# Gated attention with routed experts on one core: the first batch's queries by seven block products, their key-side sums on GpSimd, and bf16 products in a short wait

## The chip, the cores and the metric

The kernel runs on one core of one Trainium2 chip. Times are device microseconds (us). The median of several runs is what counts; beside it there is one profiled execution, from which all durations below are taken. Engines are named as in the profile: PE is TensorE (matmul), PEld its weight load, DVE is VectorE, ACT is ScalarE, POOL is GpSimd, SP is SyncE. "L555" is line 555 of the kernel.

## The reference

The input is x, 2 batches of 1024 tokens with 512 features, f32. Two branches start from the same layer norm, and their product is added to x:

```python
xn = _layernorm(x, axis=-1)
qkv = einsum('bsh,oh->bso', xn, w_qkv) + b_qkv          # attention, one head of 512
scores = einsum('bqh,bkh->bqk', q, k) / sqrt(512)
s = (softmax(scores) @ v) @ w_out.T + b_out
logits = xn @ router_w + router_b                       # 8 experts, the best 2 per token
h = einsum('td,edf->etf', xn, expert_w) + expert_b
combined = sum over the 2 experts of weight * silu(h)
y = xn + combined @ proj_w + proj_b
g = silu(norm_w * y / rms(y))
out = x + s * g
```

## The kernel before

**Algebra.** Scores are not made from queries and keys. The product of the two weight matrices, `wqk`, is made once (`product`, L580 on), queries are `xn` times `wqk` plus a column `u`, and the keys are `xn` itself, transposed (`xnT`, one tile for each batch). Value and output weights are multiplied together beforehand (`product_vo`), so `vo` holds values that already carry the output weights. Biases become small terms: `u` (from the query bias, through `sk`), a column of the router matrix `rw` (from the key bias, through `sq` and the products `pw`), and `vb`, the value bias times the output weights, which is added to `bo`. `weighted` makes the vectors `sq`, `sk` and `vb` as four scaled 128x512 slices summed on VectorE; `columns`, or a product with `ones`, then sums over partitions.

**Stages, in order of time.**
1. Loads; the value weights' product; layer norm of 16 token tiles (`means`, `variances`, `norm`, `turn_x`); in a loop over tiles t, `value_half` gives values and router logits. Inside that loop, at given t, stand `turn_w` (t = 8), `sk` (9), `vb` (10), `u` (11), `pvb` and the closing of the pool of raw weights (12) and the issue of the expert weights `ew` (13): 16 transfers on SP's queue and 16 on GpSimd's.
2. Routing, about 91 to 121 us: VectorE finds the two best experts of each token (`first_max`), counts tokens per expert (`both`, `upto`, `before`), gives each a row (products `pk`, `prank`), and builds one-hot tables `hsel`, `tsel`, `lsel`, whose products `ptok` give each expert slot's list of tokens, `tok`. TensorE does the products of `wqk` and the first batch's queries (`queries`, four calls) between these.
3. Experts: 39 slots of 128 tokens. Each slot is gathered (`xg`, GpSimd), put to memory and taken back (`xs`, `sz`, SP), transposed (`gT`, VectorE), multiplied (`ph`), its expert's bias `eb` added (VectorE) and passed through silu (ScalarE). The steps run ahead of a slot's product by 7, 5, 3 and 1 slots; `xg` and `sz` have four buffers, `gT` two.
4. Attention for pairs of 128 queries, already with seven block products instead of eight (`pair_scores`, `attend`).

**Order.** The order written in the program holds on every engine (`keep_order`): an instruction that waits holds up all that is written behind it on its engine. `hold(n)` writes n bf16 products of 128x256 that nothing reads. PSUM has four one-bank tiles `ps_mm` and two two-bank tiles `ps_big`.

Of the kernel before, what the change touches and what calls it, by code (L numbers as in the profile page):

```python
# [27 lines left out]
def kernel(  # L28
# [200 lines left out]
    for q in range(4):  # L229
        for j in range(KC):  # L230
            gps.tensor_copy(bqk[ts(q, QP), :, j], bqkv[ts(j, QP), 0:2, q])  # L231
    spread(gps, wZ[0], w_qkvT[:, ts(0, H)], others)
    load_x(gps, others, 2, 2)
# [4 lines left out]
    load_x(gps, others, 4, 4)  # L238
    ln_eps = const.tile([P, 1], FP, name="ln_eps")
    gps.memset(ln_eps, LN_EPS)  # L240
    rms_eps = const.tile([P, 1], FP, name="rms_eps")
    gps.memset(rms_eps, RMS_EPS)
# [3 lines left out]
    ones = const.tile([P, P], FP, name="ones")  # L246
    gps.memset(ones, 1.0)

    rb = const.tile([P, E1], FP, name="rb")
# [69 lines left out]

    def weighted(w_, bias, name):  # L320

        s_ = raw.tile([P, H], FP, tag="s", name=name, bufs=3)
        for c in range(KC):
            b_ = bias[:, c : c + 1]
            if c:
                dve.scalar_tensor_tensor(s_, w_[:, c, :], b_, s_, ALU.mult, ALU.add)
            else:
                dve.tensor_scalar(s_, w_[:, c, :], b_, None, ALU.mult)
            yield s_
# [63 lines left out]
    def turn_x(t):  # L393
        turn(xnT[t // ST][:, :, ts(t % ST, P)], x[:, t], "(i a)")
# [40 lines left out]
    norm(0)  # L435
    norm(1)
    turn_w(wqkT[:, 0:KC], wZ[0])
    product_vo(1, 0)
    turn_x(0)
    turn_x(1)  # L440
# [43 lines left out]
    pbb = ps_mm.tile([P, 512], FP, tag="mm", name="pbb")  # L484
    pe.matmul(pbb[:, 0:KC], lhsT=ones, rhs=bb, start=True, stop=True)
    dve.tensor_reduce(rb[:, E:E1], pbb[:, 0:KC], AX.X, ALU.add)
    dve.tensor_copy(rw[:, :, E], columns(sq_, "pw"))
    value_half(0, 0)
    turn_x(2)
# [10 lines left out]
    for t in range(2, NT):  # L500
# [17 lines left out]
        if t == 2:  # L518
            gps.dma_start(bo, b_out.partition_broadcast(P))
        if t == 8:  # L520
            turn_w(wqkT[:, KC:], wZ[1])
        if t == 9:
            *_, sk_ = weighted(wqkT[:, KC:], bqk[:, 0], "sk")
        if t == 10:

            *_, vb = weighted(wo, bqkv[:, 2], "vb")
        if t == 11:
            dve.tensor_copy(u, columns(sk_, "pu"))
        if t == 12:
# [15 lines left out]
    close(ln_guard)  # L545
    eb_guard, ebp = pool("eb", side="right")
    eb = ebp.tile([P, E, H], FP, name="eb")
    sp.dma_start(eb, expert_b.partition_broadcast(P))

    def queries(oc):  # L550

        ps = ps_big.tile([P, SH, 512], FP, tag="big", name=f"pq{oc}")
        for half in range(SH):
            for c in range(KC):
                pe.matmul(  # L555
                    ps[:, half, :],
                    lhsT=wqk[:, c, ts(oc, P)],
                    rhs=xnT[0][:, c, ts(half, 512)],
                    start=(c == 0),
                    stop=(c == KC - 1),  # L560
                )
        act.activation(
            qT[:, :, oc, :],
            ps.rearrange("p a (k f) -> p (a k) f", f=PW),
            AF.Identity,
            bias=u[:, oc : oc + 1],
        )

# [129 lines left out]
    product(3)  # L698
    queries(0)
    pt_ = ps_mm.tile([P, 512], FP, tag="mm", name="ptok")  # L700
    LG = 8
    for g in range(2 * NT // LG):
        lsel = rt.tile([P, LG, P], BF, tag="lsel", name=f"lsel{g}", bufs=4)
        dve.tensor_tensor(
            lsel,
            mixed.rearrange("p a i -> p (a i)").unsqueeze(1).to_broadcast([P, LG, P]),
            flat(lo)[:, ts(g, LG)].unsqueeze(2).to_broadcast([P, LG, P]),
            ALU.is_equal,
        )
        for j in range(LG):  # L710
            i = g * LG + j
            pe.matmul(
                pt_[:, : 2 * NSP],
                lhsT=lsel[:, j, :],
                rhs=tsel[:, i].rearrange("p k s -> p (k s)"),
                start=(i == 0),
                stop=(i == 2 * NT - 1),
            )
    tk = rt.tile([P, 2, NSP], FP, name="tk")
    dve.tensor_copy(tk.rearrange("p k s -> p (k s)"), pt_[:, : 2 * NSP])  # L720
# [22 lines left out]
    close(rt_guard)  # L743
    queries(1)
    pm = ps_mm.tile([P, 512], FP, tag="mm", name="pm")
# [6 lines left out]
    close(rc_guard)  # L752
    for oc in range(2, KC):
        queries(oc)

# [97 lines left out]

    for s in range(-steps[0][1], NS):
        pipeline(steps, s, NS)
        if LR <= s < LR + NT:
# [21 lines left out]

    KH = KC // 2
    SK = ST // 2  # L880
# [482 lines left out]
```

## Time and profile before

| what | value |
|---|---|
| median of 3 runs | 539.74 us (539.64 to 541.14) |
| the profiled execution | 540.82 us |
| its span, first to last instruction | 539.1 us, mean granted TensorE clock 0.995 |
| value products (`pv`, L462) | 60.9 us busy, 256 instructions |
| products of `wqk` (`pqk`, L586) | 32 instructions, 592 ns each as recorded |
| first batch's queries (`pq`, L555) | 28.1 us busy, 64 instructions |
| drains of these to `qT` (ACT, L562) | 4 of 1113 ns |
| expert products (`ph`, L814) | 120.3 us busy |
| `eb` load (SP's queue) | 2048 KB, 15.2 us from issue to landing |
| DMA, whole span | 112.37 MB, 208 GB/s |

A f32 product is two instructions on TensorE, so the 32 query products are 64. Instructions overlap: recorded lengths of TensorE are longer than the distance from one to the next, and sums are made with the distance. The chain of waits goes back from the last instruction to what released each step; a timeline row has start, length, engine, line, operation, output and inputs, shape, count, and in brackets the idle time before it with what ended it. A row by windows has busy time and count for PE, PEld, DVE, ACT and POOL, then the granted clock, the DMA share and GB/s.

### The profile page before, as it was taken

How to read it: one execution, taken by the hardware profiler on the slowest of the kernel's cores; microseconds unless marked ns; L12 is line 12 of the kernel's file. 1: busy time of each engine (PE TensorE's matmuls, PEld its weight loads, DVE VectorE, ACT ScalarE, POOL GpSimd, SP SyncE). 2: the span in 40 equal slices, each digit the busy share in tenths (PEclk: the TensorE clock that was granted, in tenths of full speed). 3: DMA queues.
4: the chain of work that ended last, by engine and by line, in shares of the span. 5: the costliest groups of instructions: out<-in, count | busy, mean ns of one | idle time of the engine just before them, and what ended most of it. 6: DMA issues, size and time to landing. Idle time of an engine off the chain costs nothing.

```text
span 539.1 us, 5950 instructions
## 1 busy us (share of the span) xinstructions
PE 527.3 (98%) x1762; PEld 322.1 (60%) x1762; DVE 311.2 (58%) x565; ACT 167.0 (31%) x316; POOL 236.0 (44%) x272
## 2 busy tenths in 40 slices
PE   7999999999999999999999999999999999999996
PEld 5778877444444444444466656756846657484585
DVE  2565652840333333333859376375697685949586
ACT  1535562211311111111333422423426234152340
POOL 8610006022234875230227445246189755464542
PEclk9989999999999999999999999999999999999999
DMA  9995339999999999994387922723625638295512
GB/s 212 206 220 127 78 79 227 275 217 336 319 338 331 359 348 338 318 290 146 125 281 234 299 83 92 273 78 123 229 78 179 230 95 297 71 312 176 187 54 78
DMA packets 89057, 112.37 MB, mean 208 GB/s; under 512 B 6849, under 2 KB 59201, under 8 KB 88897
## 3 DMA queue, kind: packets, MB, share of 16 engines
q1 hardware_dynamic: 75072, 75.51, 47.5%
q0 software_dynamic: 8192, 26.24, 16.4%
q10 hardware_dynamic: 5760, 10.23, 5.0%
q8 instruction: 15, 0.25, 0.2%
q14 instruction: 18, 0.14, 0.1%
HBM read 70.54 MB, written 41.42 MB: 208 GB/s over the span
## 4 chain that ended last, share of the span: by engine, by line
PE 87%; DVE 6%; issue 3%; DMA 2%; POOL 1%; ACT 1%; DVEq 0%; POOLq 0%
PE ph L814 20%; PE so L1147 17%; PE pp L1076 14%; PE po L1013 10%; PE pv L462 10%; PE pq L555 5%; PE pr L574 4%; PE sc L1057 3%; PE pqk L586 3%; DMA wZ<-in_L_attn_w_qkv_dram 2%; DVE sc L1082 1%; DVE pT L120 1%; ACT x L380 1%; POOL bqk L231 1%; DVE h L840 1%
## 5 line engine op out<-in xcount | busy, mean ns | idle before, releaser
L814 PE MATMUL ph<-ew,gT 128*128 x280 | 120.3, 592 | 0.0
L814 PEld LDWEIGHTS ph<-ew,gT 128*128 128x128 f32 x280 | 53.2, 190 | 66.9 <-issue 66.9
L788 POOL DMA_INDIRECT xg<-xn_d,tok x39 | 37.3, 957 | 78.2 <-DMA xs<-xg 52.2
L840 DVE TENSOR_TENSOR h<-ph,eb 128x512 f32<-128x512 f32 x39 | 26.8, 690 | 75.6 <-issue 40.4
L462 PE MATMUL pv<-rwvo,xnT 128*128 128x256 f32 (+1 forms) x256 | 60.9, 394 | 1.8 <-DVE xnT L120 1.0
L462 PEld LDWEIGHTS pv<-rwvo,xnT 128*128 128x128 f32 x256 | 48.6, 194 | 11.2 <-ACT x L380 1.4
L843 ACT ACTIVATE h<-h 128x512 f32<-128x512 f32 x39 | 24.5, 629 | 97.7 <-DVE h L840 89.0
L1013 PE MATMUL po<-pw,ct 128*128 128x512 f32 x112 | 49.2, 592 | 0.0
L975 POOL DMA_INDIRECT hg<-ho_d,posi_m x32 | 32.4, 1013 | 37.0 <-DVE nm L1041 23.4
L1044 ACT ACTIVATE pr<-sc,nm 128x1024 f32<-128x1024 f32 x16 | 18.3, 1145 | 90.7 <-DVE nm L1041 89.0
L1154 DVE TENSOR_TENSOR o<-so,o 128x256 f32<-128x256 f32 x49 | 20.0, 421 | 38.8 <-PE so L1147 25.9
L1192 POOL TENSOR_TENSOR o<-o,base 128x512 f32<-128x512 f32 x14 | 20.6, 1493 | 45.3 <-DVE o L1157 45.3
L1076 PE MATMUL pp<-xnT,qT 128*128 128x512 f32 x84 | 39.5, 592 | 0.0
L1147 PE MATMUL so<-vo,pT 128*128 128x256 f32 x168 | 38.5, 379 | 0.0
L1013 PEld LDWEIGHTS po<-pw,ct 128*128 128x128 f32 x112 | 21.3, 190 | 25.5 <-issue 25.3
L1147 PEld LDWEIGHTS so<-vo,pT 128*128 128x128 f32 x168 | 31.9, 190 | 7.3 <-issue 2.6
L120 DVE STREAM_TRANSPOSE gT<-sz 128x512 f32<-128x512 f32 x39 | 27.4, 702 | 13.4 <-DMA sz<-xs 13.4
L1082 DVE TENSOR_TENSOR sc<-pp,sc 128x512 f32<-128x512 f32 x49 | 31.6, 679 | 5.2 <-PE pp L1076 5.2
L539 POOL DMA_DIRECT2D ew<-in_L_ffn_expert_w_dram x16 | 8.7, 551 | 57.6 <-PE pvb L531 51.2
L574 PE MATMUL pr<-xnT,wqk 128*128 128x256 f32 x128 | 28.8, 381 | 0.9 <-DVE sc L1082 0.9
L120 DVE STREAM_TRANSPOSE pT<-pz 128x1024 f32<-128x1024 f32 x14 | 28.2, 2011 | 0.2 <-DMA pz<-ps 0.2
L574 PEld LDWEIGHTS pr<-xnT,wqk 128*128 128x128 f32 x128 | 24.2, 190 | 6.6 <-DVE sc L1082 2.2
(227 smaller groups left out, 819.9 us busy)
## 6 DMA issues: line engine op xcount, KB each, us to landing
xs<-xg SPq DMA_DIRECT2D x39, 256.0 KB, 4.7
sz<-xs SPq DMA_DIRECT2D x39, 256.0 KB, 4.6
ho_d<-h ACTq DMA_DIRECT2D x39, 256.0 KB, 4.7
ps<-pr SPq DMA_DIRECT2D x16, 512.0 KB, 3.3
pz<-ps SPq DMA_DIRECT2D x16, 512.0 KB, 5.7
xn_d<-x SPq DMA_DIRECT2D x32, 128.0 KB, 2.4
ew<-in_L_ffn_expert_w_dram POOLq DMA_DIRECT2D x16, 256.0 KB, 10.9
ew<-in_L_ffn_expert_w_dram SPq DMA_DIRECT2D x16, 256.0 KB, 13.6
```

The costliest lines, as they stand in the source:

```text
L120: dve.transpose(dst.rearrange(f"p j {order} -> p i j a", a=QP), z.rearrange("p i (j b) -> p i j b", b=QP),)
L462: pe.matmul(pvs[t][:, n, : HH + E1 * (1 - n)], lhsT=xnT[t // ST][:, c, ts(t % ST, P)], rhs=rwvo[:, c, cols], start=(c == 0), stop=(c == KC ...
L555: pe.matmul(ps[:, half, :], lhsT=wqk[:, c, ts(oc, P)], rhs=xnT[0][:, c, ts(half, 512)], start=(c == 0), stop=(c == KC - 1),)
L574: pe.matmul(ps[:, :PW], lhsT=wqk[:, c, ts(oc, P)], rhs=xnT[1][:, c, ts(k, PW)], start=(c == 0), stop=(c == KC - 1),)
L788: gps.indirect_dma_start(out=xg[s], out_offset=None, in_=xn_d, in_offset=bass.IndirectOffsetOnAxis(ap=tok[:, s : s + 1], axis=0),)
L814: pe.matmul(ph, lhsT=g_[:, c, :], rhs=ew[:, ds(r, 1), c, :].rearrange("p e f -> p (e f)"), start=(c == 0), stop=(c == KC - 1),)
L840: dve.tensor_tensor(h, ph, eb[:, ds(r, 1), :].rearrange("p e f -> p (e f)"), ALU.add)
L975: gps.indirect_dma_start(out=g_, out_offset=None, in_=ho_d, in_offset=bass.IndirectOffsetOnAxis(ap=posi_m[:, n, t : t + 1], axis=0),)
L1013: pe.matmul(po, lhsT=c_[:, c, :], rhs=pw[:, c, :], start=(c == 0), stop=(c == KC - 1))
L1076: pe.matmul(ps, lhsT=l_[:, c, :], rhs=r_[:, c, :], start=(c == 0), stop=(c == KH - 1))
L1082: dve.tensor_tensor(dst, ps, other, ALU.add)
L1147: pe.matmul(ps[:, :w_], lhsT=l_[:, c, :], rhs=r_[:, c, :], start=(c == 0), stop=(c == SK - 1),)
```

## The change

The first batch's queries are a product of `wqk` (512x512) and `xnT[0]` (512x1024). Cut into 2x2 blocks, it is now made from seven block products (Winograd's form): sums S1 to S4 of blocks of `wqk` and T1 on VectorE, T2 to T4 of blocks of `xnT[0]` on GpSimd, written directly behind the routing's first op; and the seven products are joined by VectorE sums in `qT`. Six of the products stand around the routing; the seventh (the second product, `p2`) stands at the head of the expert loop: ScalarE drains it into the space of `pw`, GpSimd adds it. The sums' pool `qs` takes the space that `eb` had, so `eb` is loaded after the third product and from ScalarE's queue.

Beside that: `vb` is made on GpSimd at t = 2, with separate scalings and sums; `pvb` goes from t = 12 to 6, `sk` from 9 to 10, `u` from 11 to 12. The constants `ln_eps`, `rms_eps` and `ones` are set earlier on GpSimd. The first token tile is transposed ahead of the query weights. Two `hold`s are added around the products `pw`.

```diff
@@ constants, before the first wZ loads of GpSimd's queue
+    ln_eps = const.tile([P, 1], FP, name="ln_eps")
+    gps.memset(ln_eps, LN_EPS)
+    rms_eps = ...
+    ones = const.tile([P, P], FP, name="ones")
+    gps.memset(ones, 1.0)
     spread(gps, wZ[0], w_qkvT[:, ts(0, H)], others)
...
@@ weighted(w_, bias, name, eng=dve)
+            if not c:
+                eng.tensor_scalar(s_, w_[:, c, :], b_, None, ALU.mult)
+            elif eng is dve:
                 dve.scalar_tensor_tensor(s_, w_[:, c, :], b_, s_, ALU.mult, ALU.add)
             else:
-                dve.tensor_scalar(s_, w_[:, c, :], b_, None, ALU.mult)
+                m_ = raw.tile([P, H], FP, tag="m", name=f"{name}_m{c}", bufs=2)
+                eng.tensor_scalar(m_, w_[:, c, :], b_, None, ALU.mult)
+                eng.tensor_tensor(s_, s_, m_, ALU.add)
...
     norm(1)
+    turn_x(0)
     turn_w(wqkT[:, 0:KC], wZ[0])
     product_vo(1, 0)
-    turn_x(0)
     turn_x(1)
...
     pe.matmul(pbb[:, 0:KC], lhsT=ones, rhs=bb, start=True, stop=True)
+    hold(4)
     dve.tensor_reduce(rb[:, E:E1], pbb[:, 0:KC], AX.X, ALU.add)
     dve.tensor_copy(rw[:, :, E], columns(sq_, "pw"))
+    hold(2)
     value_half(0, 0)
...
         if t == 2:
             gps.dma_start(bo, b_out.partition_broadcast(P))
+            *_, vb = weighted(wo, bqkv[:, 2], "vb", gps)
...
-        if t == 9:
-            *_, sk_ = weighted(wqkT[:, KC:], bqk[:, 0], "sk")
-        if t == 10:
-            *_, vb = weighted(wo, bqkv[:, 2], "vb")
-        if t == 11:
-            dve.tensor_copy(u, columns(sk_, "pu"))
-        if t == 12:
+        if t == 6:
             pvb = ps_mm.tile([P, 512], FP, tag="mm", name="pvb")
             pe.matmul(pvb, lhsT=ones, rhs=vb, start=True, stop=True)
             dve.tensor_tensor(bo, pvb, bo, ALU.add)
+        if t == 10:
+            *_, sk_ = weighted(wqkT[:, KC:], bqk[:, 0], "sk")
+        if t == 12:
+            dve.tensor_copy(u, columns(sk_, "pu"))
             close(raw_guard)
...
-    sp.dma_start(eb, expert_b.partition_broadcast(P))
+    A11, A12, A21, A22 = (
+        wqk[:, ds(h * KH, KH), ds(m * 2 * P, 2 * P)] for m in range(2) for h in range(2)
+    )
+    B11, B12, B21, B22 = (
+        xnT[0][:, ds(h * KH, KH), ts(n, 512)] for h in range(2) for n in range(2)
+    )
...
+    def query_products():
+        p1 = times(big(1), A11, B11)
+        for o in range(2):
+            act.copy(C11[:, o], p1[o].rearrange("p (k f) -> p k f", k=2))
+        p4 = times(mm(4), A22, T4)
+        yield
+        dve.tensor_tensor(S1, A21, A22, ALU.add)
+        dve.tensor_tensor(S2, S1, A11, ALU.subtract)
+        yield
+        dve.tensor_tensor(S3, A11, A21, ALU.subtract)
+        dve.tensor_tensor(S4, A12, S2, ALU.subtract)
+        dve.tensor_tensor(T1, by_pairs(B12), by_pairs(B11), ALU.subtract)
+        plus(C12, times(big(6), S2, T2), C11)
+        yield
+        plus(C21, times(big(7), S3, T3), C12)
+        p5 = times(big(5), S1, T1)
+        plus(C22, p5, C21, 1)
+        plus(C12, p5, C12)
+        plus(C21, p4, C21, 1)
+        plus(C12, times(big(3), S4, B22), C12, 0)
+        yield
+
+    def last_query_product(place):
+        p2 = times(big(2), A12, B21)
+        for o in range(2):
+            act.activation(place[:, o], p2[o], AF.Identity, bias=u[:, o : o + 1])
+        gps.tensor_tensor(C11, C11, by_pairs(place), ALU.add)
+
+    gps.tensor_tensor(T3, B22, B12, ALU.subtract)
+    gps.tensor_tensor(T2, T3, B11, ALU.add)
+    gps.tensor_tensor(T4, B21, T2, ALU.subtract)
...
     product(3)
-    queries(0)
+    pq = query_products()
+    next(pq)
...
+    next(pq)
...
-    queries(1)
+    next(pq)
...
-    for oc in range(2, KC):
-        queries(oc)
+    next(pq)
+    close(qs_guard)
+    eb_guard, ebp = pool("eb", side="right")
+    eb = ebp.tile([P, E, H], FP, name="eb")
+    act.dma_start(eb, expert_b.partition_broadcast(P))
...
     for s in range(-steps[0][1], NS):
+        if s == 0:
+            last_query_product(pw[:, 0:2])
         pipeline(steps, s, NS)
```

The four parts of `query_products` (up to each `yield`) stand behind `product(3)`; behind the `ptok` products; behind `tok`, the slots' experts `esl` and the tokens' weights; and behind the product `pm` with its two copies. `times` writes one block product as four f32 products (two row halves by two depth halves, 128x512 each) into two PSUM banks; `plus` adds a block to an earlier one in two halves on VectorE, with the bias column `u` where a fourth argument is given.

More of the change, by code (lines that the diff above doesn't have):

```diff
@@ L231 @@
             gps.tensor_copy(bqk[ts(q, QP), :, j], bqkv[ts(j, QP), 0:2, q])
+    ln_eps = const.tile([P, 1], FP, name="ln_eps")
+    gps.memset(ln_eps, LN_EPS)
+    rms_eps = const.tile([P, 1], FP, name="rms_eps")
+    gps.memset(rms_eps, RMS_EPS)
+    ones = const.tile([P, P], FP, name="ones")
+    gps.memset(ones, 1.0)
     spread(gps, wZ[0], w_qkvT[:, ts(0, H)], others)
@@ L238 @@
     load_x(gps, others, 4, 4)
[L239 to L242, printed above, removed]
     order = rc.tile([P, E], FP, name="order")
@@ L245 @@
         gps.memset(order[:, e : e + 1], float(E - e))
-    ones = const.tile([P, P], FP, name="ones")
-    gps.memset(ones, 1.0)
     rb = const.tile([P, E1], FP, name="rb")
@@ L315, with weighted @@
     spread(gps, wZ[1], w_qkvT[:, ts(1, H)], others)
-    def weighted(w_, bias, name):
+    def weighted(w_, bias, name, eng=dve):
         s_ = raw.tile([P, H], FP, tag="s", name=name, bufs=3)
@@ L324, in weighted @@
             b_ = bias[:, c : c + 1]
-            if c:
+            if not c:
+                eng.tensor_scalar(s_, w_[:, c, :], b_, None, ALU.mult)
+            elif eng is dve:
                 dve.scalar_tensor_tensor(s_, w_[:, c, :], b_, s_, ALU.mult, ALU.add)
             else:
-                dve.tensor_scalar(s_, w_[:, c, :], b_, None, ALU.mult)
+                m_ = raw.tile([P, H], FP, tag="m", name=f"{name}_m{c}", bufs=2)
+                eng.tensor_scalar(m_, w_[:, c, :], b_, None, ALU.mult)
+                eng.tensor_tensor(s_, s_, m_, ALU.add)
             yield s_
@@ L545 @@
     close(ln_guard)
-    eb_guard, ebp = pool("eb", side="right")
-    eb = ebp.tile([P, E, H], FP, name="eb")
-    sp.dma_start(eb, expert_b.partition_broadcast(P))
[L550 to L560, printed above, removed]
-                )
[L562 to L567, printed above, removed]
+    KH = KC // 2
@@ new lines, with by_pairs @@
+    qs_guard, qs = pool("qs", side="right")
+    qt = qs.tile([P, 3, KH, 512], FP, name="qt")
+    qw = qs.tile([P, 4, KH, 2 * P], FP, name="qw")
+    A11, A12, A21, A22 = (
[4 more added lines that the diff above has]
+    )
+    S1, S2, S3, S4 = (qw[:, i] for i in range(4))
+    T2, T3, T4 = (qt[:, i] for i in range(3))
+    def by_pairs(a):
+        return a.rearrange("p o (k f) -> p o k f", k=2)
@@ new lines, with times, big @@
+    C11, C12, C21, C22 = (
+        qT[:, ds(2 * n, 2), ds(2 * m, 2), :].rearrange("p k o f -> p o k f")
+        for m in range(2) for n in range(2)
+    )
+    T1 = C22
+    def times(banks, l_, r_):
+        for o in range(2):
+            for c in range(KH):
+                pe.matmul(
+                    banks[o], lhsT=l_[:, c, ts(o, P)], rhs=r_[:, c],
+                    start=(c == 0), stop=(c == KH - 1),
+                )
+        return banks
+    def big(name):
+        ps = ps_big.tile([P, 2, 512], FP, tag="big", name=f"pq{name}")
+        return [ps[:, o, :] for o in range(2)]
@@ new lines, in mm, with plus @@
+    def mm(name):
+        return [ps_mm.tile([P, 512], FP, tag="mm", name=f"pq{name}_{o}") for o in range(2)]
+    def plus(dst, banks, other, m=None):
+        for o in range(2):
+            ps = banks[o].rearrange("p (k f) -> p k f", k=2)
+            if m is None:
+                dve.tensor_tensor(dst[:, o], ps, other[:, o], ALU.add)
+            else:
+                dve.scalar_tensor_tensor(
+                    dst[:, o], ps, u[:, 2 * m + o : 2 * m + o + 1], other[:, o],
+                    ALU.add, ALU.add,
+                )
@@ new lines, in query_products @@
+    def query_products():
+        p1 = times(big(1), A11, B11)
+        for o in range(2):
+            act.copy(C11[:, o], p1[o].rearrange("p (k f) -> p k f", k=2))
[16 more added lines that the diff above has]
+        yield
@@ L569, in queries_of @@
+    def last_query_product(place):
+        p2 = times(big(2), A12, B21)
+        for o in range(2):
+            act.activation(place[:, o], p2[o], AF.Identity, bias=u[:, o : o + 1])
[3 more added lines that the diff above has]
+    gps.tensor_tensor(T4, B21, T2, ALU.subtract)
     def queries_of(k, bank):
@@ L867 @@
     close(ew_guard)
-    KH = KC // 2
     SK = ST // 2
```

## The prediction

> **What bounds the kernel now.** I read the busy table first, then the chain of waits, then the timeline of each engine around every edit.
>
> ```profile
> PE 527.3 (98%) x1762; PEld 322.1 (60%) x1762; DVE 311.2 (58%) x565; ACT 167.0 (31%) x316; POOL 236.0 (44%) x272
> ```
>
> TensorE sets the end; whatever shortens its list, or makes it wait, moves the time one for one unless slack takes it up. The chain shows the routing and query stage and the two other places touched (start, length, instructions):
>
> ```profile
> 32.00 7.19 PE pv L462 x24
> ...
> 71.05 0.63 DVE xnT L120
> 71.68 0.14 issue
> 71.81 3.75 PE pv L462 x16
> ...
> 98.25 0.12 PE pk L640 x2
> 98.37 0.32 PE prank L642 x2
> 98.69 0.22 PE prank L643 x2
> 98.91 6.87 PE pqk L586 x16
> 105.78 6.87 PE pq L555 x16
> 112.65 1.15 PE ptok L712 x32
> 113.80 6.94 PE pq L555 x16
> 120.74 0.17 PE pm L746 x2
> 120.91 13.79 PE pq L555 x32
> ```
>
> From 91 to 244 TensorE has no gap, so the queries are paid in full: 16 instructions take 6.87 us, 0.429 each. VectorE's routing ops run beside the products, but only just ahead; GpSimd issues expert weights until shortly before. From their two timelines:
>
> ```profile
> 96.15 0.38 DVE L628 TENSOR_TENSOR both<-hot 128x128 f32<-128x128 f32 x1
> 96.63 0.42 DVE L634 TENSOR_TENSOR_SCAN upto<-carry,both 128x128 f32<-128x128 f32 x1
> 97.08 0.29 DVE L636 TENSOR_TENSOR before<-upto,both 128x128 f32<-128x128 f32 x1
> ...
> 95.76 0.55 POOL L539 DMA_DIRECT2D ew<-in_L_ffn_expert_w_dram  x1 [1.71 <-DMA ew<-in_L_ffn_expert_w_dram]
> 115.24 1.06 POOL L788 DMA_INDIRECT xg<-xn_d,tok  x1 [18.93 <-DVE npast L733]
> ```
>
> `upto` is ready at 97.05 and wanted at 98.25, `before` at 97.37 and wanted at 98.69: slack of 1.2 and 1.3 us. GpSimd is idle from 96.3 to 115.2; there the new sums go. Last, what a clash costs (a later stage's timeline) and the clock by stretches (busy per engine, then granted clock):
>
> ```profile
> 395.92 2.93 POOL L928 TENSOR_TENSOR xnT<-vo 128x512 f32<-128x512 f32 x2
> 395.95 3.45 DVE L989 SCALAR_TENSOR_TENSOR hg<-hg,wgt_m,hg 128x512 f32<-128x512 f32 x2
> ...
> 32.00:33.00 1.00, 1.00 (x2) 0.84 (x3) 0.00 (x0) 1.00 (x4) 0.00 (x0) 0.50 1.10 248
> ```
>
> **The queries.** Seven block products of 8 instructions replace eight: 64 - 56 = 8 x 0.429 = **-3.44 us**. Seven drains with sums replace four ScalarE drains of 1.11. VectorE gets 12 half sums from PSUM (L1082: 0.68 each, 0.60 apart), S1 to S4 (0.65 each, half of L928's 1.22 for 128x1024) and T1 (1.22): some 11 us from the slot tables to the experts, 18 us long. Followed product by product (order 1, 4, 6, 7, 5, 3, 2), the sixth's drain frees its PSUM buffer 0.5 to 0.9 us before the fifth needs it, the fifth's 0.5 us before the second's, and the last sum ends some 1.7 us before the first expert product, where the first `gT` transpose (0.71) must still fit: cost 0, up to 1 if durations stretch. The second product, at the head of the experts, is counted in the 56. Its addition on GpSimd (2.5) holds up gather 7 and those queued behind it; slot 7's product comes 24 us later: 0.
>
> **The three sums T3, T2, T4 on GpSimd.** Each has 128x1024 elements; 128x512 takes 1.28 there (L859), so 2.5 each, 7.5 in a row. They follow the last `ew` issue (96.31). The row above says what they do to VectorE: the 128x512 op with two SBUF inputs, 0.743 at its shortest, takes 1.73 when GpSimd sums run, while sums with one input in PSUM keep 0.68. Taken as an added 1.0 per op, three ops lose 3.0, which slack cuts to 1.7. The Trainium skill (SBUF — State Buffer, Who interferes with whom) has a harder rule: a VectorE op with two SBUF inputs and a GpSimd op that reads SBUF exclude each other for the whole instruction. Then the loss grows with GpSimd's instruction: three of 2.5, some 6 to 7 us on a chain with 1.3 of slack. By the row this term is +1.7 and the whole near the old time; by the rule it is +4 to +6, slower. I take the rule, since in the row each op ends about 0.55 after the GpSimd op that it met.
> Its working, all ahead by 0.99 (next part): `both` runs from 95.16 to 95.5 and T3, issued at 95.3, from then to 98.0; `upto` waits and ends at 98.4; T2 to 100.9; `before` ends at 101.2; T4 to 103.7. TensorE wants pk at 97.26 and gets past `prank` at 101.5 instead of 97.9: 3.6. Behind them the slot tables end 5.7 later, at 116.5, when the `ptok` products want the last at 116.2: 0.3. Sum **+3.9**; +5.9 if T3 starts 0.4 earlier and catches `both` too; 0 at the lower end.
> A stall of 4 us has a second price, the **clock**. In the windows, it falls to 0.50 at 31.9 and stays 3.4 us there, after TensorE had been only sparsely busy; 24 value products took 7.19 instead of 5.6 (x8 takes 1.87 elsewhere). The skill (TensorE: Matmul & The Clock Gate, Part 1) lets the clock fall after a window of about 3.4 us idle. Here the longest gap before the fall was 0.92, so sparse windows are enough. For 4 us of waiting both say that it falls: **+1.6** (0 to 2).
>
> **`sk` and `vb`.** Before 71.81 TensorE waits 0.99 for the transpose that queues behind `sk` (2.8 us of VectorE). `sk` goes a tile later, `vb` (2.8) to GpSimd, `pvb` from tile 12 to 6 (same 0.86). The transpose of tile 11 then ends some 0.6 ahead of its product, tile 12's, behind `sk`, likewise: **-0.99**, 0 at worst. But `vb` on GpSimd starts near 30 behind the `bo` load: four scalings of 1.8 (on the line through 128x32 0.32, L225, and 128x128 0.62, L299; bounds 1.28 and 2.5) and three sums of 1.28: 11 us. The first scaling can start when the last `sq` sum, also of two inputs, lets go (30.4), and holds to 32.2; VectorE's `shift` op (two inputs, due at 31.0) waits for it, and behind `shift` are queued the copy of the key bias's column, which TensorE awaits at 32.0, and the next transposes: **+0.6** (0 to 1.8). The tail of `vb` then meets the three `dev` ops at 39.6; they have 0.8 of slack before the product of their squares, and wait about twice that: **+0.8** (0 to 4). The addition to `bo` (0.69 on VectorE) now stands before tile 8's transpose, which ends at 58.0 for a product at 59.7: 0. Gathers are not near.
>
> **The start.** `ln_eps` set early ends ScalarE's wait of 1.16, and tile 0's transpose precedes the weights', which wait for their load until 21.85: only 0.3 of VectorE's chain to 32.0 fits in front: **-0.3**. The moved memsets delay GpSimd's first `wZ` loads by 0.2, inside DMA that is saturated: 0.
>
> **The bf16 products.** Four take 0.6 in an idle 0.92, two 0.2 in 0.26: no cost. If they keep the clock up: -1.6; but then the `dev` ops come 1.6 earlier and meet more of `vb` (+1.3). I count -0.1. By the skill's idle rule they gain nothing, having no such gap to fill.
>
> **`eb` on ScalarE's queue after the third product.** Before, it was issued at 111.78 on SP and took 15.2 to land, between `ew` and the gathers. Now these gathers go first, and `eb` leaves when the third product ends, 3.4 ahead of the first expert product. Slot 2's transpose is queued behind slot 0's bias addition, so `eb` is in time if it lands within 3.44 + 6.87 (two slots' products) - 1.5 (that addition and that transpose) = 8.8 us. Its 2 MB at the 391 GB/s moved from 120 to 123 is 5.4, plus some 3 of latency (3.3, the shortest landing of `ew`): 8.4. **0**, up to 3; ScalarE has nothing else waiting behind the issue.
>
> **Sum** against the profiled execution (540.82, its span 539.1 plus 1.7 around it): -3.44 - 0.99 + 3.9 + 1.6 + 0.6 + 0.8 - 0.3 - 0.1 = +2.1, so 542.9. That execution lies 1.1 above the median, 539.74; one half-clock window, which another execution may escape, is worth that. I take half of it off: **542.4**.
>
> **Rivals.**
> (A) As summed, 0.53: 540.5 to 545.
> (B) Faster, 0.22: the sums don't hold up the routing. One mechanism, at `upto`/`before`: GpSimd and VectorE share better than by exclusion, or T3 comes when the chain's two-input ops are past. It decides where the hold-up of `before` stays under 1.3, and the clock then isn't lost: -3.44 - 0.99 + 1.0 around the start + 0.3 = -3.1, about 536.7. For it: the sums' window is otherwise idle. Against: the row at 395.95.
> (C) No change, 0.12: without that hold-up the experts begin 4.4 sooner, at 130.3, and the gathers cannot follow: slot 0's `sz` was turned at 132.15, slot 12's transpose waited for its landing until 173.5 and ended 1.6 before its product. DMA is saturated from 84 on and `eb`'s bytes are only moved. TensorE then waits 2 to 3: 538.5 to 540.5.
> (D) Worse, 0.13: T3 catches `both`, scalings cost 2.5, and the clock falls twice: 545 to 548.
> If the bf16 products don't hold the clock, which the change says they are for, nothing but the -0.1 changes.
>
> **Numbers.** About 0.3% (1.6 us) is what a measurement here can tell from no change. Slower than 541.4: 0.43 of A and all of D, 0.56. Within: 0.10 of A, C and the slow edge of B, 0.24. Faster than 538.1: B, 0.20. The range leaves out the tail of B below 536.5 and most of D: 536.5 to 545.8.
>
> **What would show it.** Right: `pk` and `prank` together wait for VectorE by 3 us or more; `upto` and `before` last over 2 us instead of 0.4; clock 0.50 behind; 56 `pq` instructions at 0.429; no wait before 71.8; `dev` ops longer. Wrong: routing ops at old lengths beside GpSimd's sums (B); transposes of `gT` waiting for `sz`, or first bias additions for `eb` (C).

## The result, and the profile after

The changed kernel takes **546.94 us** in the median of four runs (544.17, 544.67, 549.22, 549.69), the kernel before 540.33 beside it: ratio 1.0122, interval 1.0086 to 1.0158. It is slower by about 6.6 us, and its own times lie in two groups 5 us apart. The profiled execution is of the lower group: 544.67 us, span 543.0, so 3.9 more than the 539.1 of before. A later execution (run `after_again`, below) is of the upper group. The ratios leave out disturbed executions, over 1.5% above the fastest of the same kernel: in what follows two of eb_s0's six, of which its profile is one.

The busy table first, to be held against the line of before: two instructions fewer on TensorE for the same busy time, and more work on VectorE and GpSimd.

```profile
PE 527.5 (97%) x1760; PEld 322.3 (59%) x1760; DVE 326.3 (60%) x578; ACT 165.1 (30%) x316; POOL 256.0 (47%) x283
```

TensorE has 8 query instructions less, and 6 bf16 ones more. Busy time is no help here: a product at half clock counts as busy for longer (24 value products took 7.19 in before, with the half clock in them, and 5.57 here). The chain of waits tells where the time goes (start, length, what). In the routing, where before there were only products, it now runs through VectorE:

```profile
93.43 2.73 DVE upto L701
...
96.19 2.26 DVE before L703
...
98.49 0.49 PE prank L710 x2
98.98 8.56 PE pqk L653 x16
```

`upto` took 0.42 before and takes 2.73; `before` took 0.29 and takes 2.26. Behind them the sixteen `pqk` instructions, which were 6.87, take 8.56. The timelines of VectorE, GpSimd and TensorE in that stretch (start, length, engine, line, operation, and in brackets the idle time with what ended it) say why:

```profile
93.43 2.72 DVE L701 TENSOR_TENSOR_SCAN upto<-carry,both 128x128 f32<-128x128 f32 x1
96.19 2.25 DVE L703 TENSOR_TENSOR before<-upto,both 128x128 f32<-128x128 f32 x1
98.36 0.15 DVE L714 TENSOR_SCALAR cnt<-pk 128x8 int32<-128x8 f32 x1
98.55 2.19 DVE L715 TENSOR_SCALAR cnt<-cnt 128x8 int32<-128x8 int32 x1
...
93.50 2.36 POOL L632 TENSOR_TENSOR qt<-xnT 128x1024 f32<-128x1024 f32 x1
```

```profile
96.21 0.39 PE L707 MATMUL pk<-upto,ones 128*128 128x8 f32 x2 [1.15 <-DVE upto L701]
98.49 0.49 PE L710 MATMUL prank<-before,ones 128*128 128x128 f32 x2 [1.57 <-DVE before L703]
```

T3 runs from 93.50 to 95.86, T2 from 95.94 to 98.28 and T4 from 98.36 to 100.71. In each, one VectorE operation is caught and ends 0.03 to 0.3 behind it; between two sums VectorE gets through to the next operation, which is caught again. Even `cnt` at L715, with a single input, is held for 2.19 us; `cnt` at L714, whose input is PSUM, is not. The second stretch that was gapless before is the head of the experts. The chain of before, then that of the changed kernel:

```profile
134.69 109.88 PE ph L814 x256
```

```profile
129.75 9.67 DMA eb<-in_L_ffn_expert_b_dram
...
139.44 0.02 SPq L116
...
139.48 3.09 DMA sz<-xs
...
142.66 0.72 DVE gT L120
...
143.43 2.80 PE ph L886 x3
```

`eb` takes 9.67 us to land. SP's queue stands still until then, though `sz` has nothing to do with `eb`: in the trace both transfers count on the same semaphore (106), and SP's wait for it ends at 139.44, when `eb` has landed (139.42). So 4.01 us pass from `eb`'s landing to slot 2's product (143.43): issue, `sz` and transpose. SP's own timeline shows the hole, VectorE's when the first bias addition had its data, and TensorE's what it waited:

```profile
128.83 0.36 SPq L112 DMA_DIRECT2D xs<-xg  x1
139.48 0.33 SPq L116 DMA_DIRECT2D sz<-xs  x1
```

```profile
139.51 0.69 DVE L912 TENSOR_TENSOR h<-ph,eb 128x512 f32<-128x512 f32 x1 [6.87 <-DMA eb<-in_L_ffn_expert_b_dram]
```

```profile
143.43 7.11 PE L886 MATMUL ph<-ew,gT 128*128 x12 [3.54 <-DVE gT L120]
```

Last, the clock by stretches (busy time of PE, PEld, DVE, ACT and POOL, then granted clock, DMA share, GB/s):

```profile
31.90:32.90 1.00, 1.00 (x6) 0.84 (x5) 0.26 (x1) 1.00 (x3) 1.00 (x1) 1.00 1.05 231
99.30:102.60 3.30, 3.30 (x5) 1.29 (x4) 3.02 (x8) 0.00 (x0) 1.41 (x1) 0.50 1.05 277
143.60:147.00 3.40, 3.40 (x5) 1.34 (x6) 1.06 (x2) 0.63 (x1) 1.19 (x2) 0.50 1.10 363
```

The half clock at 31.9 is gone; two new stretches of 3.41 us have come, one behind each stall.

**One table for all kernels.** Four marks on TensorE cut the span: the first `pqk` instruction, the first `pq`, the first `ph`, the first `sc` (attention). What follows `sc` is 282.9 to 283.2 in every kernel. Each figure is a difference from before (91.22, 14.40, 28.91, 121.40), read from the first starts in the one profiled execution of each:

| run | to `pqk` | `pqk` to `pq` (routing) | `pq` to `ph` (queries) | `ph` to `sc` (experts) | span |
|---|---|---|---|---|---|
| changed kernel | -3.2 | +4.9 | -3.4 | +5.5 | 543.0 |
| after_again | -1.3 | +7.3 | -3.4 | +7.4 | 549.1 |
| start_only | -1.6 | 0 | 0 | 0 | 537.6 |
| queries_only | -0.8 | +7.3 | -3.4 | +4.9 | 547.0 |
| holds_only | +0.3 | 0 | 0 | 0 | 539.4 |
| idle_sums | -3.2 | +7.5 | 0 | 0 | 543.4 |
| idle_sets | -3.4 | 0 | 0 | +1.3 | 537.0 |
| start_eb | -2.7 | 0 | 0 | 0 | 536.4 |
| eb_s0 | +2.2 | +4.7 | -3.4 | +6.1 | 548.7 |
| eb_pool | -2.3 | +7.8 | -3.4 | +5.3 | 546.4 |
| no_clash | -0.9 | 0 | -2.9 | +6.3 | 541.4 |
| best_clash | -3.0 | +7.3 | -2.4 | +0.5 | 541.5 |
| best | -2.2 | 0 | -2.6 | +0.2 | 534.3 |

### The profile page after: what moved, and what is told of

It is laid out like the page before. It is cut to its first block, busy times and chain, and to the rows that moved or that the text cites. A ratio compares the mean times of both kernels' runs of the same rounds, so it can differ in the third digit from the quotient of the medians.

```text
span 543.0 us, 5979 instructions
## 1 busy us (share of the span) xinstructions
PE 527.5 (97%) x1760; PEld 322.3 (59%) x1760; DVE 326.3 (60%) x578; ACT 165.1 (30%) x316; POOL 256.0 (47%) x283
## 4 chain that ended last, share of the span: by engine, by line
PE 73%; DVE 6%; DMA 2%; issue 2%; ACT 0%; DVEq 0%; ACTq 0%; SPq 0%
PE ph L886 19%; PE so L1220 17%; PE pp L1149 14%; PE po L1086 10%; PE pr L641 4%; PE pq L578 4%; PE sc L1130 3%; DMA eb<-in_L_ffn_expert_b_dram 2%; PE pqk L653 2%; DVE sc L1155 1%; DVE pT L120 1%; DMA sz<-xs 1%; DVE h L912 1%; DVE upto L701 1%; DVE wqk L1227 0%
## 5 line engine op out<-in xcount | busy, mean ns | idle before, releaser
L886 PE MATMUL ph<-ew,gT 128*128 x280 | 122.3, 599 | 3.5 <-DVE gT L120 3.5
L465 PE MATMUL pv<-rwvo,xnT 128*128 128x256 f32 (+1 forms) x256 | 58.9, 386 | 0.1
```

The source lines that it names most:

```text
L465: pe.matmul(pvs[t][:, n, : HH + E1 * (1 - n)], lhsT=xnT[t // ST][:, c, ts(t % ST, P)], rhs=rwvo[:, c, cols], start=(c == 0), stop=(c == KC ...
L886: pe.matmul(ph, lhsT=g_[:, c, :], rhs=ew[:, ds(r, 1), c, :].rearrange("p e f -> p (e f)"), start=(c == 0), stop=(c == KC - 1),)
```

## The experiments

The theory after the result: the queries save what was forecast; two costs that are independent of each other outweigh it, the hold-up of the routing by the three sums and the lateness of `eb`. Rivals: the start's edits lose what they gain (by `vb` on GpSimd); the seven products stall in themselves; `eb` is only late because of where it stands in a queue.

### Halves of the change: start_only, queries_only, and the changed kernel again

start_only has every edit but the queries' (and `eb`'s); queries_only has the queries' and `eb`'s edits and nothing else.

```diff
 start_only:   + ln_eps, rms_eps, ones early; turn_x(0) first; hold(4), hold(2);
               + vb on GpSimd at t = 2; pvb at 6; sk at 10; u at 12
 queries_only: + query_products, last_query_product, T3 T2 T4 on GpSimd, eb on ACT's queue
```

> The kernel before with every edit of the change except the queries and the load of eb: early constants, tile 0's transpose first, the two holds, vb on GpSimd, sk and pvb moved. Theory 1 (the start's edits gain on their own what the traces show at 88 us, and nothing gives it back later): 3.2 us faster than before in an execution whose clock falls at 32 us in before, about 2 to 3 in the median, so 537 to 538; clock 1.00 from 7 to 540 us, no wait of TensorE before 88. Rival (the 3.2 us are used up again at the experts, since the gathers end when the DMA lets them): within 1 us of before, with gT transposes that wait for sz.

Measured: 539.04 us, ratio 0.9982 (0.9970 to 0.9994): a gain of 1.3, less than was expected, and its profile still has a half-clock stretch, from 31.44.

> The kernel before with the block products, GpSimd's sums and eb on ScalarE's queue, without the start's edits. Theory 1: -3.4 for the products, +3.3 for pk and prank held up by the locked-out upto and before, +1.7 for a half-clock window behind it, +3.5 and +1.7 for slot 2 behind eb: 6 to 8 us slower than before, 546.5 to 548.5 in the better executions, and the same two long VectorE ops of 2 us and more. Rival (the loss comes from the start's edits moving the routing against the expert weights' loads): no such hold-up, no slower than before.

Measured: 550.76 us, ratio 1.0208 (1.0184 to 1.0233): slower than was expected, since three VectorE operations were caught and not two; TensorE waited 5.12 for `upto`.

> The changed kernel once more, for its spread: its four executions were 544.2, 544.7, 549.2 and 549.7, with mean clocks of 0.993, 0.994, 0.986 and 0.985. Theory 1 (the two levels differ by where the 3.4 us clock windows lie against TensorE's waits, so that more windows at half clock follow the waits): again two levels some 5 us apart, and every higher one has the lower mean clock; if the profiled execution is a high one, it shows two or three more half-clock windows than the 99.2 and 143.6 of the first. Rival (the higher level has a longer landing of eb or another wait): a high execution with the same clock windows and a longer wait.

Measured: 548.91 us, ratio 1.0135 (1.0101 to 1.0169). Both of what was expected came together: more half-clock stretches and longer waits.

So the loss lies wholly in the queries' half, and the start's edits gain a little: no wait before 71.8 any more, and TensorE waits only 0.16 for a `dev` that `vb` holds up. `after_again`'s profile is of the upper group. On VectorE, and T3 on GpSimd:

```profile
94.50 2.29 DVE L681 TENSOR_TENSOR hot<-key,km 128x128 f32<-128x128 f32 x1
...
96.82 2.48 DVE L695 TENSOR_TENSOR both<-hot 128x128 f32<-128x128 f32 x1
99.41 2.37 DVE L701 TENSOR_TENSOR_SCAN upto<-carry,both 128x128 f32<-128x128 f32 x1
...
94.27 2.35 POOL L632 TENSOR_TENSOR qt<-xnT 128x1024 f32<-128x1024 f32 x1
```

And its windows behind the two stalls:

```profile
99.40:106.10 6.70, 4.27 (x10) 2.73 (x11) 5.78 (x17) 0.01 (x1) 2.09 (x1) 0.50 1.05 268
147.20:153.90 6.70, 5.30 (x7) 2.20 (x8) 2.00 (x3) 0.63 (x1) 2.23 (x3) 0.50 1.08 355
```

Here T3 comes two operations earlier in the chain. All three sums catch operations that `pk` waits for (`hot`, `both`, `upto`) instead of two, TensorE waits 4.90 in one piece, and the clock is at half for two stretches of 3.41 instead of one, in both places; `eb` takes 10.84 us. Of the 6.1 us between the two profiles, 2.4 are the routing and 1.9 the experts; the other 1.8 lie before `pqk`, where this execution waits longer for its loads and first column. What the sums catch depends on when GpSimd's last `ew` issue ends against VectorE's chain; that issue waits for earlier `ew` loads to land (0.63 us in the changed kernel's profile).

### Is it the sums, and is it that they read? idle_sums, idle_sets

start_only, with the three sums added and nothing made of them; and the same with fills in their place.

```diff
 idle_sums:  + gps.tensor_tensor(T3, B22, B12, ALU.subtract)
             + gps.tensor_tensor(T2, T3, B11, ALU.add)
             + gps.tensor_tensor(T4, B21, T2, ALU.subtract)
 idle_sets:  + for t_ in (T3, T2, T4):
             +     for _ in range(2):
             +         gps.memset(t_, 0.0)
```

> The kernel start_only (all edits but the queries and eb; 539.0 us) with the change's three GpSimd sums added at their place, written into the space where eb is loaded afterwards, so that nobody reads them; queries and eb as before. Theory 1 (VectorE ops with two SBUF inputs and the sums exclude each other, one whole GpSimd op of 2.35 us each): three VectorE ops of 2.2 to 2.7 us instead of 0.3 to 0.4, TensorE waits 2.7 to 5 us before pk or prank and runs one or two half-clock windows behind it: 4 to 8 us slower than start_only, 543 to 547. Rival (the sums share the port and the waits in the changed kernel come from something else in its routing): routing ops at 0.3 to 0.4, time within 1 us of start_only.

Measured: 544.69 us, ratio 1.0087 (1.0057 to 1.0118); the clock is at 0.50 for 6.83 us behind the wait. Two of the three caught operations, and TensorE's wait:

```profile
92.62 2.57 DVE L625 TENSOR_TENSOR hot<-key,km 128x128 f32<-128x128 f32 x1
...
97.82 2.37 DVE L645 TENSOR_TENSOR_SCAN upto<-carry,both 128x128 f32<-128x128 f32 x1
```

```profile
100.24 0.59 PE L651 MATMUL pk<-upto,ones 128*128 128x8 f32 x2 [5.19 <-DVE upto L645]
```

> The start's edits alone, and in place of the three GpSimd sums six fills with zeros of the same three spaces (128x1024 each, results unread): the same place in GpSimd's order and the same bytes written, but nothing read from SBUF. If VectorE is held up by exclusion against GpSimd instructions that read SBUF: routing ops upto and before at 0.3 to 0.5 us, no wait of TensorE at pk or prank, and a time within 1 us of the start's edits alone (539.0), against 544.7 with the sums. If any long GpSimd instruction on SBUF holds VectorE up: ops of 1 to 2.5 us again, and 542 to 545.

Measured: 538.05 us, ratio 0.9974 (0.9961 to 0.9988). VectorE and GpSimd at the place of the clash:

```profile
92.77 0.38 DVE L639 TENSOR_TENSOR both<-hot 128x128 f32<-128x128 f32 x1
93.25 0.42 DVE L645 TENSOR_TENSOR_SCAN upto<-carry,both 128x128 f32<-128x128 f32 x1
93.70 0.29 DVE L647 TENSOR_TENSOR before<-upto,both 128x128 f32<-128x128 f32 x1
...
95.43 0.88 DVE L661 CAST nsl<-cnt 128x8 f32<-128x8 int32 x1
...
96.76 0.56 DVE L666 TENSOR_SCALAR first<-first 128x8 f32<-128x8 f32 x1
...
93.39 5.83 POOL L558 MEMSET eb<- 128x1024 f32 x6
```

Sums whose results nobody reads cost 5.6 us (544.69 against 539.04), and fills of the same spaces at the same time cost nothing: `before`, which starts 0.31 into the first fill, keeps its 0.29, and so do the operations with two inputs behind it. So for operations with two inputs the hold-up comes with what GpSimd reads, not with its running. Three operations with one input do stretch beside the fills: the cast `nsl<-cnt` (0.88 for the 0.17 it takes elsewhere), `first` (0.56 for 0.17) and a second cast (0.35 for 0.18). Each ends 0.02 to 0.03 behind the end of a fill. TensorE waits for none of them.

### Is eb late because of a queue? eb_s0, eb_pool

Two attempts to leave the sums and free SP's queue: the load written later, and issued by GpSimd.

```diff
 after the fourth part of query_products:
-    act.dma_start(eb, expert_b.partition_broadcast(P))
 in the slot loop, s == 0, ahead of last_query_product:
+    act.dma_start(eb, expert_b.partition_broadcast(P))      # eb_s0
+    gps.dma_start(eb, expert_b.partition_broadcast(P))      # eb_pool
```

> The changed kernel with one line moved: the load of eb is written at slot 0 of the expert loop instead of ahead of the loop. ScalarE's queue has nothing between the two places, so it is issued at the same time (about 129.7). Theory 1 (SP's queue stood still from 129.2 to 139.4 because its next load uses the same DMA semaphore as eb and so must wait for eb to land; the order of writing deals these out): SP issues slot 2's sz at about 129 to 130, TensorE's wait before slot 2 falls from 3.5 to 0 to 1.5 us, and with it the half-clock window behind it can go: 3 to 5 us faster than the changed kernel, 540 to 542 in its better executions. Rival A (eb's 2 MB take the DMA engines from slot 2's transfers): sz is issued early but lands as late as before, 142 or later, wait unchanged. Rival B (slot 0's bias addition waits for eb at 139.4 and slot 2's transpose is queued behind it): the wait falls only to 1 us and not below.

Measured: 546.2 us over all six executions, ratio 1.0085 (1.0052 to 1.0118). It did not separate the theories: `eb` counted on the same semaphore as before, and SP stood still again, from 133.83 to 145.29, with a wait of 4.38 before slot 2.

> The changed kernel with the load of eb issued by GpSimd at slot 0 of the expert loop, behind seven gathers, instead of by ScalarE; moving the line alone (eb_s0) had left eb on the same DMA semaphore, and SP stood still as before. GpSimd's loads have semaphores of their own. Theory 1 (SP stands still only because of the shared semaphore): SP issues slot 2's sz within 1 us of its xs landing, at least 5 us before eb lands; TensorE's wait before slot 2 is then set by slot 0's bias addition and the transpose behind it, some 1.5 us after eb's landing: 1 to 2.5 us instead of 3.5 to 4.5; the whole 1.5 to 4 us faster than the changed kernel. Rival (eb's 2 MB starve slot 2's transfers): sz issued early, landing only after eb has, wait unchanged.

Measured: 547.2 us, ratio 1.0125 (1.0099 to 1.0151). From its chain, and SP's timeline below it:

```profile
133.84 11.60 DMA eb<-in_L_ffn_expert_b_dram
...
145.53 0.06 DVE h L911
...
146.14 0.71 DVE gT L120
...
146.90 3.33 PE ph L885 x4
```

```profile
133.77 0.46 SPq L116 DMA_DIRECT2D sz<-xs  x1
```

SP is free now: slot 2's `sz` is issued at 133.77, before `eb`. Still TensorE waits 3.31 before slot 2. The `sz` landed only at 143.51, 9.7 us later, where the first five of the kernel before took 2.7 to 4.4; and `eb` took 11.6, so that slot 0's bias addition, with slot 2's transpose queued behind it on VectorE, came at 145.53. It is this addition that ends last: 1.46 us pass from `eb`'s landing (145.44) to slot 2's product. So the theory that the shared semaphore alone is at fault has fallen. It is one of two ways to the same wait: 2 MB put beside the gathers at that point are late themselves and make the gathers late.

### Taking the two costs out: no_clash, best, best_clash, start_eb

no_clash makes the three sums on VectorE at t = 14, before the routing, in the space of the last two experts' weights; their loads follow on ScalarE's queue when the products have used the sums. best has this and loads `eb` at t = 8, into the space of the first eight token tiles. best_clash is best with the sums on GpSimd behind the last early `ew` issue again; four of the early `ew` loads go from SP's queue to GpSimd's with them. start_eb is start_only with the early `eb`.

```diff
 no_clash, in the value loop:
+            for e in range(E - 2):
+                load_ew(e, (sp, sp, gps, gps))
+            T3, T2, T4 = ew[:, E - 1, 0:KH], ew[:, E - 1, KH:KC], ew[:, E - 2, 0:KH]
+        if t == 14:
+            dve.tensor_tensor(T3, B22, B12, ALU.subtract)
+            dve.tensor_tensor(T2, T3, B11, ALU.add)
+            dve.tensor_tensor(T4, B21, T2, ALU.subtract)
 behind product 4 and behind product 7:
+        load_ew(E - 2, (act,) * 4)
+        load_ew(E - 1, (act,) * 4)
 best, besides (x is laid over eb for its first eight tiles):
+        if t == 8:
+            sp.dma_start(eb, expert_b.partition_broadcast(P))
 best_clash, against best:
-            dve.tensor_tensor(T3, ...) and the other two, at t == 14
+    gps.tensor_tensor(T3, ...) and the other two, where the change has them
-                load_ew(e, (sp, sp, gps, gps))
+                load_ew(e, (sp, gps if e < 4 else sp, gps, gps))
```

> The changed kernel with T2 to T4 made by VectorE at tile 14 (78 to 88 us, where it is idle), in the space of the last two experts' weights, whose loads go to ScalarE's queue behind the fourth and the seventh product. No GpSimd sums beside the routing; eb as in the change. Theory 1: routing ops at 0.3 to 0.4, no wait before pk and prank, no half-clock window at 99; the wait before slot 2 stays or grows (eb is late against experts that begin 5 to 9 us sooner): 4 to 7 us faster than the changed kernel, 540 to 543. Rival (the routing was bound by VectorE's own added sums): pk or prank still wait, less than 2 us faster.

Measured: 543.61 us, ratio 1.0078 (1.0049 to 1.0106). The routing is back at its old length to the hundredth (14.40). Then its chain:

```profile
121.10 7.12 DMA ew<-in_L_ffn_expert_w_dram
...
128.24 0.03 SPq L116
...
128.29 9.89 DMA sz<-xs
...
138.21 0.72 DVE gT L120
...
138.98 3.39 PE ph L893 x4
```

The same pattern a slot earlier, and now with an `ew` load of ScalarE's queue in front of SP's issue (both on semaphore 108): TensorE waits 4.49 before slot 1, `eb` takes 10.75 us. With the clash taken away, most of what is left is the head of the experts, +6.3; the two experts' late `ew` loads are part of it.

> no_clash, and eb loaded early: it takes the space of the first eight token tiles' x, dead after 60 us, and is loaded by SP at tile 8, when the DMA engines are a third busy. Theory 1: neither wait is left, TensorE's list is 3.4 us shorter than start_only's: 3 to 4 us faster than start_only, 535 to 536.5, experts beginning at about 129.5 without a wait before slot 2. Rival (C of the prediction: the gathers cannot follow experts that begin so early): waits of gT transposes for sz of 1.5 to 3 us in slots 0 to 3 or 12, 537.5 to 539.

Measured: **536.02 us**, ratio 0.9931 (0.9912 to 0.9951): faster than both kernels. `eb`, issued at 60.07, landed at 67.39. The chain:

```profile
96.06 0.12 PE pk L722 x2
...
96.73 6.87 PE pqk L668 x16
103.60 6.87 PE pq L594 x16
...
113.06 4.80 DMA xg<-xn_d,tok
...
117.87 5.12 DMA xs<-xg
...
123.13 5.88 DMA sz<-xs
...
129.03 0.72 DVE gT L120
...
129.80 4.56 PE ph L898 x10
```

Where TensorE set the end throughout before, slot 0's gather is now last: gather, store and load come to 15.8 us from the tokens' list on, and TensorE waits 0.72 for them, 0.88 by the starts. That is why the queries' column shows -2.6 instead of -3.4. The late `ew` loads of the last two experts move beside these transfers.

> The kernel with early sums and early eb (536.0), with T3, T2 and T4 put back on GpSimd behind its last ew issue, where the change has them (GpSimd issues 16 of the 24 early ew loads, so that it comes to them at about the same time). One edit: the clash, without eb's lateness. If the clash costs what the sums cost on top of the start's edits (5.6 us, with a stall of 5 at pk and two clock windows), 541 to 542; if it falls on the lighter pattern of the changed kernel (waits of 1.15 and 1.57, one window of 1.7), 538.5 to 540. Rival: with eb out of the way the waits of slot 0 for its gathers take up what is lost in the routing, and 536 to 537.5 remains.

Measured: 543.7 us, ratio 1.0077 (1.0057 to 1.0098). The three sums caught `hot`, `both` and `upto` (2.57, 2.49 and 2.36 us), TensorE waited 5.18, and the clock was at half for 6.83. The edit costs 7.7 us, more than either figure that was expected. TensorE still waits for slot 0's transpose (0.84), though the experts begin 6.6 us later than in best. In both kernels slot 0's gather, store and load take 16 us, about the time from the gather's issue to the product that wants them. In the changed kernel, with as much time left, the same three took 10.9 (116.92 to 127.79), and it has no late `ew` loads beside them. So these loads account for the wait better than the kernel's speed does; no run takes them out alone.

> The start's edits, the queries as before in eight block products, and eb loaded at t = 8 into the space of the first eight token tiles. In the kernel before eb already lands (127.0) ahead of its first use, so loading it early should give 0: 538.5 to 539.5. Then the 3 us by which the kernel with early sums and early eb (536.0) beats the start's edits alone (539.0) are the seventh-product form's own saving. Rival: eb out of the gathers' way lets the first slots' transfers land sooner and gives 1 to 2 us by itself: 537 to 538.

Measured: 538.24 us, ratio 0.9979 (0.9964 to 0.9993), against 539.04 (0.9970 to 0.9994) without: no difference that the intervals show. So best's gain over it, 2.2 us, is that of the seven products, with their sums early on VectorE and the late `ew` loads they bring.

The four kernels with the seven products and the start's edits lie at 536.0 (neither cost), 543.6 (only `eb` late), 543.7 (only the clash) and 546.9 (both); the first three have the late `ew` loads, the last has not. Each cost alone is worth 7.6 to 7.7; together they cost 10.9 in the median, not 15. The profiles show why: no_clash is 7.1 above best, best_clash 7.2, and after_again, which catches three operations as best_clash does, is 14.8 above it, near the sum. The lower group catches two that matter (+4.9 for +7.3) and gets to `pqk` sooner, and is 8.7 above. The upper group, 549.5 in the mean of its five times, is 13.5 above best's median.

### What the bf16 products do: holds_only

```diff
     pe.matmul(pbb[:, 0:KC], lhsT=ones, rhs=bb, start=True, stop=True)
+    hold(4)
     dve.tensor_reduce(rb[:, E:E1], pbb[:, 0:KC], AX.X, ALU.add)
     dve.tensor_copy(rw[:, :, E], columns(sq_, "pw"))
+    hold(2)
```

> The kernel before with the six bf16 products alone. If they keep the clock at full rate in some executions: 0.3 to 1.6 us less, more than the others of the start's edits give. If, as in the profile of the start's edits alone, the clock falls at 31.4 all the same: within 0.3 us of before (540.3), nothing to tell.

Measured: 539.57 us, ratio 0.9997 (0.9985 to 1.0008): no difference that can be told by the time. In its profile the clock falls all the same:

```profile
31.50:34.80 3.30, 3.28 (x14) 2.44 (x14) 1.82 (x9) 3.12 (x8) 0.00 (x0) 0.67 1.07 235
```

It fell too in the profiles of start_only and no_clash, and not in those of start_eb, idle_sets and best, which have the same bf16 products. The mean clock recorded for each execution says roughly how often: in the profiles without a fall there and without later stalls it is 0.999 or more, in those with one 0.995 or 0.996. It is 0.997 or more in 22 of 78 executions of the kernel before, taken beside these runs, in 8 of 14 of holds_only, and in 45 of 62 of start_only, start_eb and idle_sets, which have the other edits of the start as well. So the products seem to make the fall rarer, on few executions, and don't prevent it; at 1.7 us each (half of 3.41), some 0.5 to 0.8 us in the mean, which the times can't tell from nothing.

## Why the prediction was wrong

Forecast: 542.4, range 536.5 to 545.8, slower the likeliest at 0.56. Slower was right, the size was not. The step that failed is `eb`, put at 0: it cost 5.5 in one profile and 7.4 in the other. The three sums failed in their count: the case with three caught operations was a side case and is the commoner one. By the prediction's own steps:

**The queries, -3.44.** Right: -3.43 from the first `pq` to the first `ph`, in every kernel where nothing else is waited for. The drains, the sums on VectorE and the PSUM buffers held TensorE up nowhere. The "sixth's drain" and its neighbours were timed well enough to be hidden.

**Exclusion or slowing.** The prediction weighed a row (a VectorE operation gets 1.0 longer beside GpSimd's sums) against the Trainium skill (SBUF — State Buffer, Who interferes with whom), and took the rule. The rule held: each caught operation lasts as long as what is left of the GpSimd sum, 2.2 to 2.8 us. The same section says that an instruction that only writes doesn't block one with two inputs, which idle_sets shows (`before` 0.29), and that casts and scalar operations on one input can, in some modes, collide with GpSimd even so, which fits the casts and `first` beside the fills (0.88, 0.35, 0.56) and `cnt` at 2.19. The prediction looked at two-input operations only and took `cnt` for free; here that cost nothing, since the `ptok` products waited for no table.

**The three sums, +3.9 and +1.6 of clock.** For the lower group the mechanism is as worked out: `upto` behind T3, `before` behind T2. By the starts of the products it is 1.32 + 1.73 of waiting (1.15 and 1.57 as recorded), 0.2 in the small products between, and 1.7 of clock: 4.9 against 5.5. What failed is the sentence "+5.9 if T3 starts 0.4 earlier and catches `both` too", held as a side case and given to rival D at 0.13. The catching of three operations that TensorE waits for is the commoner case: it is in the profiles of after_again, queries_only, idle_sums, best_clash and eb_pool, and five of the eight executions of the changed kernel lie in the upper group (of which one has a profile). The chain's place against the last `ew` issue was forecast to some tenths, from one execution, where more than that moves: `pqk` begins between 88.0 and 89.9 in two executions of the same kernel. And the second half-clock stretch belongs to it: the routing costs +7.3 then, not 5.5.

**`eb`, "0, up to 3".** This step failed outright: +5.5 in the lower group, 3.70 of waiting by the starts (3.54 as recorded) and 1.7 of clock behind it; 7.4 in the upper. Two of its terms were off.
- *The path behind the landing, 1.5.* The deadline of 8.8 us counts a bias addition and a transpose behind it. But slot 2's `sz` was issued only when `eb` had landed, so that 4.01 us passed from the landing to the product. With that path the deadline is 6.3 us (3.44 + 6.87 - 4.0), and the forecast landing of 8.4 would have missed it too. queries_only shows it: there `eb` landed in 8.90, near the forecast, and TensorE waited 3.09. The 1.5 holds where SP is free (1.46 in eb_pool).
- *The landing, 8.4.* It took 9.67, and 8.9 to 11.6 over the runs that load `eb` there. It was sized as its own bytes at the whole bandwidth plus a latency, as though nothing else were moving, in a stage that the same prediction called saturated. In a quieter stretch it does land in 7.3 (best); before, beside the `ew` loads, it took 15.2, and this row was read as the exception rather than as the warning.

So of the 4.1 us between the 0.4 of slack that was forecast and the 3.7 of waiting, 2.5 are the path, 1.3 the landing, and 0.3 a later issue. Two things were left out altogether: that SP's issue can wait for a landing of ScalarE's queue, and that the other slots' transfers get late beside `eb` (an `xs` of 8.7 in the changed kernel, an `sz` of 9.7 in eb_pool). The price of a stall, a half clock behind it, had been put to the routing and not here.

**`sk` and `vb`, the start.** Better than forecast. The wait before 71.8 is gone, as worked out (-0.99). `vb` on GpSimd took 10.3 us, near the 11 that were estimated, but `shift` took 0.30 and the first `dev` 0.53, and TensorE waited for neither: the terms +0.6 and +0.8 are 0 in this profile. That is in part luck: in best `vb` stretched two `dev` operations to 1.05 and 0.63, and TensorE waited 0.40. The fall at 31.9, put at -0.1, is gone in the profiled execution (-1.6); whether by the bf16 products or by chance one execution can't say. In the medians the start is worth 1.3 to 2.1 (start_only, start_eb, idle_sets), where the prediction's terms made it 0.

**Rival C** (the gathers can't follow a faster kernel) is small: 1.05 at slot 12 in idle_sets, the slot that it named. The 0.72 before slot 0 in best is no clear case of it, since it comes with late `ew` loads. **Rival B**'s chance of 0.20 was too much beside a rule that spoke against it.

The sum for the profiled execution: -3.2 - 3.4 + 4.9 + 5.5 = +3.8 of the +3.9. Forecast for it was +2.1; without `eb` it would have been -1.7. That the forecast lies within 2 us of this execution is luck: `eb` missed by 5.5 one way, the start by 3.2 the other. The upper group's profile has less of that: -1.3 - 3.4 + 7.3 + 7.4 = +10.0.

## What to carry to other kernels

Work given to an idle GpSimd is free only where VectorE's chain beside it isn't awaited: here each GpSimd sum, which reads SBUF, held up one VectorE operation until its own end. So ask which operation each will catch, in the worst alignment and not the one of a single profile. A load moved later into a stage of gathers was late itself, made the gathers late, and held another engine's queue; look for a hole in time for it far ahead, at the price of some space. And a stall of TensorE was paid twice: behind seven stalls of 2.5 to 4.5 us lay one half-clock stretch of 3.4 us (1.7 more), behind six of 4.5 to 5.2 us two.

## What the runs showed of the hardware beyond that

- **How the clock falls behind a stall.** In the profiles of this case, every fall behind a stall came with 1.7 to 3.4 us of idle TensorE in the 3.41 us before it. In the next 3.41 us, 1.5 to 3.0 of idle kept the clock down for as long again (six times), and 0.6 or less let it rise (seven times). At 31 to 33 us it fell with only 0.6 to 1.2 of idle (1.8 once) among small products, and with 0.6 did not fall in the profiles of best, start_eb and idle_sets; in eb_s0 it stayed down there for two stretches, with no idle in the first. So idle time alone does not decide it.
- **A wait across queues.** A transfer of SP's queue was issued only when a transfer of ScalarE's queue with the same semaphore had landed: SP stood still for 10.3 us here, and 11.5 in eb_s0. Moving the load's line by one slot did not change which semaphore it got.
- **One input can be enough.** `cnt`, 128x8 int32 in SBUF, one input, was held for 2.19 us by a GpSimd sum, and the cast behind it took 0.88 beside GpSimd's fills, which only write; with PSUM as the input the same kind of operation kept its 0.15 beside the start of that sum.
